# Indexed stores of routed outputs, and a written order from the last dense blocks through the second attention

## The chip, the cores and the metric

The kernel runs on one core of one Trainium2 chip. A core has five engines that run at the same time: TensorE (PE in the profile, with PEld for its weight loads), VectorE (DVE), ScalarE (ACT), GpSimd (POOL) and SyncE (SP), and 16 DMA engines that all of them share. Each engine works through its own queue in order and waits on semaphores that other engines or transfers raise. The metric is the time of one execution on the device in microseconds (us); the median of three runs before the change is 994.7 us.

## The reference, cut to what matters

Two layers of a gated cross-attention block with mixtures of experts, on 16 sequences of 112 tokens of width 256, in fp32. What the change touches is the end of the first layer's feed-forward and the second layer's attention:

```python
x = x + tanh(g_xattn[0]) * L0_xattn(layernorm(x), ctx)
x = x + tanh(g_ffn[0]) * L0_ffn(layernorm(x))     # 14 routed experts, top 2, and 2 shared ones
x = x + tanh(g_xattn[1]) * L1_xattn(layernorm(x), ctx)
x = x + tanh(g_ffn[1]) * L1_ffn(layernorm(x))

def _L0_ffn_ref(x, router_w, rms_w, w1, w2, rms_w_s, w1_s, w2_s):
    gates = softmax(xf @ router_w);  top_v, top_i = top_k(gates, 2)
    masked = zeros.at[rows, top_i].set(top_v);  masked = masked / (masked.sum(-1) + EPS)
    # _ffn: silu(rmsnorm(x) * rw @ W1) @ W2, with W1 256x512 and W2 512x256
    routed_out = einsum('end,ne->nd', vmap(_ffn)(rms_w, w1, w2), masked)
    shared = vmap(_ffn)(rms_w_s, w1_s, w2_s).sum(0)
    return routed_out + shared

def _L1_xattn_ref(x, ctx, ...):          # one head of 256, 112 queries on 375 keys
    attn = softmax((x @ Wq.T + bq) @ (ctx @ Wk.T + bk).T * scale)
    return (x + attn @ (ctx @ Wv.T + bv)) @ Wo.T + bo
```

## The kernel before

The 1792 tokens lie in 14 token tiles of 128 (`NT`), each a row of `x_sb[:, i, :]`, which holds the running sum x on the chip. Tokens normalized and turned (width on the partitions) stand in `xT`. The program has these stages in order.

The first attention ends with a norm per token tile (`normed1`), whose rows go to a table in DRAM, `xn_rows`, beside being turned into `xT`. It is put down in a written order: inside `tc.manual_schedule()` each engine's instructions keep the order of the program text. Everything after it, up to the end, is ordered by a scheduler that places instructions by its own estimates; SP's, POOL's and all other queues are then fixed in that order.

The routed stage sorts the 3584 token-expert pairs by expert into 41 tiles of 128 slots (`TILES0`), each tile of one expert, with the last slots of an expert's last tile and the tail tiles empty. `places` gives for each token the two slots (`at_i`) and for each tile its expert (`owner_i`); `takers` gives for each slot its token, through a matrix product of one-hot rows (0 where a slot is empty). While these are worked out, PE does three units of the two shared experts ("dense" units: an expert `e`, a first token tile `t0`, a width of 4 or 2 tiles; `hidden_piece` makes one of four 128-row pieces of the hidden layer, `output_piece` the output of one token tile and adds it to `x_sb`).

A routed tile `t` then takes: a load of the expert's weights (`wr_sb`, 1025 KB, four buffers, SP's queue), a gather of its tokens' rows (`xg_sb`, an indirect DMA from POOL's queue, four buffers), two PE transposes (`px`), DVE's scaled copy `xgT`, 16 matmuls and a SiLU on ACT (`routed_hidden`), matmuls into `pyr`, DVE's copy `yr` (three buffers), and a plain store of 128 KB to the tile's own slice of a DRAM table `yg` on SP's queue. PE works on the hidden layer of tile t before the output of tile t - 1, and the gather and turn of tile t + 1 before both.

Then come the four dense units that are left (`rest`, two of four token tiles, two of two), with `combine` between them: for each token tile two indirect gathers from `yg` on POOL's queue (`yb`, eight buffers), one for each of the token's two slots, each followed by a DVE instruction that adds the gated rows to `x_sb`, and then the tile's mean and variance (`stats_of`). After all 14, `power` on POOL makes the reciprocal roots of all tiles at once (`rstd2`).

The second attention begins with products of its weights (`product`, `column`, and rows of the biases through `spread`), then `transposed` normalizes and turns all token tiles in pairs, and `add_bias_rows` adds the output bias to `x_sb` on POOL. The loop over the sequences has, in step n, `scores1(n)`, the loads of context n + 2, `apply1(n - 2)`, query products for the next four sequences, `project1` for token tiles that are complete, and `turn1(n - 1)`; `scores1` ends with the division by the softmax sum. The last stage, four experts on all tokens, begins with the same bulk norm and turn (`mv3`, `rstd3`).

The indexed gather that the sum uses today:

```python
nc.gpsimd.indirect_dma_start(
    out=y, out_offset=None, in_=yg,
    in_offset=bass.IndirectOffsetOnAxis(ap=at_i[:, i, r : r + 1], axis=0),
)
```

Of the kernel before, what the change touches and what calls it, by code (L numbers as in the profile page):

```python
# [8 lines left out]
F32 = mybir.dt.float32  # L9
I32 = mybir.dt.int32  # L10
# [41 lines left out]
def tile_flamingo(  # L52
# [103 lines left out]

    tokens_i = const.tile([P, NT], I32, tag="tokens_i", name="tokens_i")
    nc.gpsimd.iota(tokens_i, pattern=[[P, NT]], base=0, channel_multiplier=1)
    tokens = const.tile([P, NT], F32, tag="tokens", name="tokens")
    nc.vector.tensor_copy(tokens, tokens_i)  # L160
    dram = ctx.enter_context(tc.tile_pool(name="dram", bufs=1, space=bass.MemoryType.DRAM))
    xn_rows = dram.tile([N, D], F32, tag="xn_rows", name="xn_rows")
    yg = dram.tile([TILES0 * P, D], F32, tag="yg", name="yg")
    tg = const.tile([P, 4], F32, tag="tg", name="tg")
# [47 lines left out]
    def top2(pool, logits, e, tiny, scale):  # L212
# [34 lines left out]
        if scale is not None:  # L247
            nc.vector.tensor_scalar(sm, sm, scale, None, ALU.mult)
        gates = pool.tile([P, NT, 2], F32, tag=f"gates{e}", name="gates", bufs=1)
        for r in range(2):  # L250
# [68 lines left out]
    def takers(wk, pool, tag, at_i, e, n):  # L319


        def full(name, shape, dtype=F32):
            return wk.tile(shape, dtype, tag=f"{name}{e}", name=name, bufs=1)

        parts = []
        for name, op, by in (("lane", ALU.bitwise_and, P - 1), ("tile", ALU.arith_shift_right, 7)):
            t_i = full(f"{name}_i", [P, NT, 2], I32)
            nc.vector.tensor_scalar(t_i, at_i, by, None, op)
            t = full(name, [P, NT, 2])
            nc.vector.tensor_copy(t, t_i)  # L330
            parts.append(t)
        lane, tile_ = parts
        number = full("number", [P, NT, 2, n])
        sh = [P, NT, 2, n]
        nc.vector.tensor_tensor(
            number, marks[:, :n].unsqueeze(1).unsqueeze(1).to_broadcast(sh), bc(tile_, sh), ALU.is_equal
        )
        nc.vector.tensor_tensor(
            number, number, tokens.unsqueeze(2).unsqueeze(3).to_broadcast(sh), ALU.mult
        )  # L340
        pn = pool.tile([P, n], F32, tag=tag, name="pn")
        for i in range(NT):
            here = wk.tile([P, 2, P], F32, tag="here", name="here", bufs=3)
            for r in range(2):
                nc.vector.tensor_scalar(here[:, r, :], lanes, lane[:, i, r : r + 1], None, ALU.is_equal)
            for r in range(2):
                nc.tensor.matmul(
                    pn, here[:, r, :], number[:, i, r, :],
                    start=(i == 0 and r == 0), stop=(i == NT - 1 and r == 1),
                )  # L350
        taker = full("taker", [P, n], I32)
        nc.vector.tensor_copy(taker, pn)
        return taker

# [78 lines left out]
    with tc.tile_pool(name="a0", bufs=2) as a0, tc.tile_pool(  # L433
# [338 lines left out]
    with tc.tile_pool(name="f0", bufs=3) as f0, tc.tile_pool(  # L772
# [40 lines left out]
        def routed_out(t, w, hT):  # L813
# [27 lines left out]

        def combine(i):
            for r in range(2):
                y = f0.tile([P, D], F32, tag="yb", name="yb", bufs=8)
                nc.gpsimd.indirect_dma_start(
                    out=y, out_offset=None, in_=yg,
                    in_offset=bass.IndirectOffsetOnAxis(ap=at_i[:, i, r : r + 1], axis=0),
                )
                nc.vector.scalar_tensor_tensor(
                    x_sb[:, i, :], y, gates[:, i, r : r + 1], x_sb[:, i, :], ALU.mult, ALU.add  # L850
                )
            stats_of(mv2, i, x_sb[:, i, :])

        units = [(e, t0, w) for t0, w in blocks for e in range(ES)]
# [9 lines left out]
        run(first, route)  # L864
        (at_i, owner_i), taker = found["at"], found["taker"]

# [11 lines left out]

        done = 0

        def added(n):

            nonlocal done
            while n > 0 and done < rest[n - 1][1]:
                combine(done)
                done += 1

        run(rest, added)
        while done < NT:
            combine(done)  # L890
            done += 1

# [3 lines left out]
    rstd2 = by_token("rstd2")  # L896
    power(rstd2, mv2[:, :, 1], EPS, -0.5)
    mv3 = mv_tile("mv3")
    with tc.tile_pool(name="a1", bufs=2) as a1, tc.tile_pool(
        name="a1_mm", bufs=3, space=PSUM  # L900
    ) as ps_mm, tc.tile_pool(name="a1_s", bufs=2, space=PSUM) as ps_s, tc.tile_pool(
        name="a1_t", bufs=1, space=PSUM
    ) as ps_t, tc.tile_pool(name="a1_o", bufs=2, space=PSUM) as ps_o:
        oT = keep.tile([P, KD, N], F32, tag="oT", name="oT1")
        rows_c = {}
# [31 lines left out]
        def spread(bias):  # L937
# [4 lines left out]
            return t  # L942

        for b in range(2):
            context(b)
            context_rows(b)
        wqk = product("wqk", wq1_sb, wk1_sb)
        wvo = product("wvo", wv1_sb, wo1_sb)
# [16 lines left out]

        xT = transposed(ps_mm, "mm", mv2, rstd2)
        add_bias_rows(1)

        G = 4
        qts = {}  # L970

        def queries1(b0, c):
# [3 lines left out]
            for k in range(KD):  # L976
                nc.tensor.matmul(
                    pq, wqk[:, k, c * P : (c + 1) * P], xT[:, k, b0 * TQ : (b0 + G) * TQ],
                    start=(k == 0), stop=(k == KD - 1),
                )  # L980
# [4 lines left out]
        def scores1(b):  # L985
            ps = ps_s.tile([TQ, 512], F32, tag="s", name="ps1")
            t0 = (b % G) * TQ
            for k in range(KD):
                nc.tensor.matmul(
                    ps[:, S : S + 1], xT[:, k, b * TQ : (b + 1) * TQ], wqb[:, k : k + 1],  # L990
                    start=(k == 0), stop=(k == KD - 1),
# [43 lines left out]
        def project1(i):  # L1035
            po = ps_mm.tile([P, D], F32, tag="mm", name="po1")
            cut = slice(i * P, (i + 1) * P)
            for n, (a, w) in enumerate(((xT, wo1_sb), (oT, wvo))):
                for k in range(KD):
# [263 lines left out]
```

## Time and profile before

| what | value |
|---|---|
| median of three runs | 994.7 us (990.64 to 995.96) |
| the profiled execution: time | 990.7 us |
| its span, first to last instruction | 989.0 us |
| mean granted TensorE clock in it | 0.980 |
| PE busy | 928.2 us (94%) |
| DVE, ACT, POOL busy | 493.9, 320.3, 184.8 us |
| routed tiles on PE, about | 404.7 to 573.5 us |
| rest of dense blocks | 573.3 to 629.4 us |
| products, norm, turn | 629.2 to 651.7 us |
| second attention | 651.7 to 737.5 us |
| last stage | 738 us to the end |

The span is shorter than the time by 1.7 us, which lie before the first and after the last instruction. Times of stages are read from PE's timeline, counted from the start of the span. "Busy" of PE counts a matmul at half clock like one at full clock, so a busy PE can still be slow; the granted clock of each stretch says which it is. An engine's idle time is listed with what ended it, its releaser; a releaser that the trace doesn't have is called "remote" or "another core or an unknown queue". The profile's row for the routed gathers (op count, busy time and mean ns, then idle time and what ended it) shows the form in which such groups are given:

```profile
L786 POOL DMA_INDIRECT xg_sb<-xn_rows,taker x41 | 39.0, 952 | 165.6 <-PE px L793 121.4
```

### The profile page before, as it was taken

How to read it: one execution, taken by the hardware profiler on the slowest of the kernel's cores; microseconds unless marked ns; L12 is line 12 of the kernel's file. 1: busy time of each engine (PE TensorE's matmuls, PEld its weight loads, DVE VectorE, ACT ScalarE, POOL GpSimd, SP SyncE). 2: the span in 40 equal slices, each digit the busy share in tenths (PEclk: the TensorE clock that was granted, in tenths of full speed). 3: DMA queues.
4: the chain of work that ended last, by engine and by line, in shares of the span. 5: the costliest groups of instructions: out<-in, count | busy, mean ns of one | idle time of the engine just before them, and what ended most of it. 6: DMA issues, size and time to landing. Idle time of an engine off the chain costs nothing.

```text
span 989.0 us, 18177 instructions
## 1 busy us (share of the span) xinstructions
PE 928.2 (94%) x7306; PEld 666.2 (67%) x7306; DVE 493.9 (50%) x1281; ACT 320.3 (32%) x723; POOL 184.8 (19%) x325
## 2 busy tenths in 40 slices
PE   6999999999999789999989996999989999999995
PEld 3566666666666457888878854768876666766664
DVE  4666665555566165222222233644445655465674
ACT  3555555555554330111111120142223221222222
POOL 3232221111111201222212054410015000000043
PEclk9999999999999999999999997889998999999998
DMA  6400001110110005499999822334400000000011
GB/s 244 161 3 22 23 23 34 33 39 1 59 39 23 11 6 192 130 314 330 303 319 284 296 83 88 127 92 158 124 18 1 0 22 22 1 1 0 1 35 40
DMA packets 34307, 91.51 MB, mean 93 GB/s; under 512 B 4288, under 2 KB 17984, under 8 KB 28976
## 3 DMA queue, kind: packets, MB, share of 16 engines
q1 hardware_dynamic: 30368, 80.79, 24.7%
q0 software_dynamic: 3312, 9.05, 3.2%
q8 instruction: 57, 0.93, 0.4%
q10 hardware_dynamic: 544, 0.52, 0.2%
q14 instruction: 26, 0.21, 0.1%
HBM read 81.31 MB, written 9.04 MB: 91 GB/s over the span
## 4 chain that ended last, share of the span: by engine, by line
PE 82%; DMA 8%; DVE 3%; ACT 3%; another core or an unknown queue 2%; issue 1%; POOL 0%; POOLq 0%; DVEq 0%; ACTq 0%
PE ph L1130 10%; PE py L1160 9%; DMA wr_sb<-in_wr_dram 8%; PE pt L573 6%; PE pt L592 6%; PE pt L472 5%; PE sp L545 5%; PE phr L805 5%; PE pyr L817 4%; PE ph L407 4%; PE py L417 3%; PE sp L485 3%; PE po L1040 2%; PE ps L994 2%; PE pa L1029 2%
## 5 line engine op out<-in xcount | busy, mean ns | idle before, releaser
L552 DVE TENSOR_REDUCE mz<-sp 112x2 f32<-112x750 f32 x128 | 114.2, 934 | 55.7 <-PE sp L545 55.7
L580 ACT ACTIVATE pT<-pt 125x336 f32<-125x336 f32 x256 | 94.6, 456 | 65.0 <-PE pt L573 65.0
L1130 PE MATMUL ph<-w1b_sb,xT 128*128 128x512 f32 x224 | 102.1, 600 | 0.0
L1160 PE MATMUL py<-w2b_sb,hT 128*128 128x256 f32 x448 | 100.8, 382 | 0.0
L805 PE MATMUL phr<-xgT,wr_sb 128*128 128x128 f32 x656 | 82.5, 279 | 11.4 <-DVE xgT L795 11.3
L1160 PEld LDWEIGHTS py<-w2b_sb,hT 128*128 128x128 f32 x448 | 82.2, 190 | 14.0 <-ACT hT L1152 4.2
L805 PEld LDWEIGHTS phr<-xgT,wr_sb 128*128 128x128 f32 x656 | 77.2, 191 | 15.3 <-DVE xgT L795 15.1
L795 DVE TENSOR_SCALAR xgT<-px,wr_sb 128x128 f32<-128x128 f32 x82 | 24.9, 346 | 109.2 <-DMA wr_sb<-in_wr_dram 93.9
L817 PE MATMUL pyr<-wr_sb,hTr 128*128 128x256 f32 x328 | 77.4, 379 | 0.0
L810 ACT ACTIVATE hTr<-phr 128x512 f32<-128x512 f32 x41 | 24.5, 597 | 155.5 <-PE phr L805 155.5
L1130 PEld LDWEIGHTS ph<-w1b_sb,xT 128*128 128x128 f32 x224 | 41.7, 191 | 42.4 <-issue 38.7
L786 POOL DMA_INDIRECT xg_sb<-xn_rows,taker x41 | 39.0, 952 | 165.6 <-PE px L793 121.4
L188 POOL TENSOR_SCALAR rstd<-mv 128x1 f32<-128x1 f32 (+2 forms) x23 | 5.2, 228 | 338.4 <-DVE mv L181 338.4
L592 PEld LDWEIGHTS pt<-pT,va 125*32 125x32 f32 x1536 | 38.0, 109 | 39.1 <-ACT pT L580 33.6
L817 PEld LDWEIGHTS pyr<-wr_sb,hTr 128*128 128x128 f32 x328 | 59.3, 190 | 6.4
L573 PE MATMUL pt<-qm,kt 32*125 32x112 f32 x1536 | 61.2, 283 | 0.7 <-ACT kt L477 0.4
L592 PE MATMUL pt<-pT,va 125*32 125x112 f32 x1536 | 58.7, 264 | 2.0 <-ACT pT L580 2.0
L573 PEld LDWEIGHTS pt<-qm,kt 32*125 32x125 f32 x1536 | 49.1, 183 | 15.7 <-issue 11.6
L1137 ACT ACTIVATE rh<-mvh,eps 128x1 f32<-128x1 f32 x56 | 16.3, 292 | 131.4 <-DVE mvh L181 131.3
L545 PE MATMUL sp<-kt,qt 32*112 32x375 f32 x512 | 55.9, 488 | 1.2 <-ACT qt L504 0.8
L472 PE MATMUL pt<-ctx_sb,wk 128*128 128x375 f32 x128 | 50.3, 516 | 5.8 <-DMA ctx_sb<-in_ctxT_dram 5.8
L417 PE MATMUL py<-w_sb,hT 128*128 128x256 f32 x192 | 44.3, 390 | 7.2 <-issue 7.2
(241 smaller groups left out, 1447.5 us busy)
## 6 DMA issues: line engine op xcount, KB each, us to landing
wr_sb<-in_wr_dram SPq DMA_DIRECT2D x41, 1025.0 KB
ctx_sb<-in_ctxT_dram SPq DMA_DIRECT2D x32, 375.0 KB
ctxn_sb<-in_ctxN_dram SPq DMA_DIRECT2D x16, 375.0 KB
yg<-yr SPq DMA_DIRECT2D x41, 128.0 KB
w1b_sb<-in_w1b_dram SPq DMA_DIRECT2D x4, 512.0 KB
w2b_sb<-in_w2b_dram SPq DMA_DIRECT2D x4, 512.0 KB
xn_rows<-xn SPq DMA_DIRECT2D x14, 128.0 KB
out_dram<-yf SPq DMA_DIRECT2D x14, 128.0 KB
```

Of the source, the lines that this page charges most:

```text
L407: nc.tensor.matmul(ph, a[:, k, m * P : (m + 1) * P], xT[:, k, t0 * P : (t0 + n) * P], start=(k == 0), stop=(k == KD - 1),)
L417: nc.tensor.matmul(py, hT[:, m, j * P : (j + 1) * P], c[:, m, :], start=(m == 0), stop=(m == KH - 1),)
L472: nc.tensor.matmul(pk, wk0_sb[:, k, c * P : (c + 1) * P], ctxs[b][:, k, :], start=(k == 0), stop=(k == KD - 1),)
L545: nc.tensor.matmul(sps[j // 2][:TQ, j % 2, :S], qt[r : r + HP, c, t0 : t0 + TQ], kt[r : r + HP, g, u, :], start=True, stop=True,)
L552: nc.vector.tensor_reduce(mz[:, 2 * h : 2 * h + 2, HD * (1 - u)], sp[:TQ, :, :S], AX.X, ALU.max, negate=True,)
L573: nc.tensor.matmul(sts[j][:SC, s * TQ : (s + 1) * TQ], kt[r : r + HP, c // 2, c % 2, s * SC : (s + 1) * SC], qm[r : r + HP, :], start=True ...
L580: nc.scalar.activation(pT[:, j, :], sts[j][:SC, : NSC * TQ], AF.Exp)
L592: nc.tensor.matmul(po[r : r + HP, :], va[:, s, (c // 2) * 8 + j * 2 + c % 2, :], pT[:, j, s * TQ : (s + 1) * TQ], start=(s == 0), stop=(s ...
L805: nc.tensor.matmul(ph[:, m, :], a[:, k, m * P : (m + 1) * P], xgT[:, k, :], start=(k == 0), stop=(k == KD - 1),)
L817: nc.tensor.matmul(py, hT[:, m, :], c[:, m, :], start=(m == 0), stop=(m == KH - 1))
L1130: nc.tensor.matmul(ph, xT[:, k, i * P : (i + 1) * P], a[:, k, :], start=(k == 0), stop=(k == KD - 1),)
L1160: nc.tensor.matmul(py, hT[:, m, j * P : (j + 1) * P], c[:, m, :], start=(m == 0), stop=(m == KH - 1),)
```

## The change

There are three parts.

Routed outputs are stored by index. A table `pairs` holds, for token n and choice r, the number 2n + r + 1; `takers` now yields `slot`, this number for each slot (0 for an empty one), and from it `taker`, the token plus one. `xn_rows` gets a row 0 of zeros for empty slots, its tokens move down by one row. The output of a routed tile goes to `y_rows` at the rows `slot` names, by an indirect DMA from POOL's queue in place of SP's plain store; empty slots all write row 0. The two rows of a token then lie beside each other, and `combine` loads those of a whole token tile with one plain DMA of 256 KB on SP's queue (`yb`, now 2 KB per partition, six buffers).

The rest of the dense units, the sums, the norms and the second attention stand in one written order, within `tc.manual_schedule()`. The products and bias rows come first. Then the dense pieces follow in the order hidden 0, hidden 1, output 0, output 1, hidden 2, hidden 3, output 2, output 3 (28 pieces), and after every second piece from the third on a `tick(c)`: sum and root of token tile c, norm of tile c - 1 on DVE, turn of tile c - 2 on PE with ACT's copy and POOL's bias add. Ticks 13 to 15 come among the first two query products. The turned tokens stand in `xs`, in the buffer of `oT`, since `xT` is still read by the dense pieces; `oT` takes that of `xT`.

In the attention's loop the division by the softmax sum leaves `scores1` and becomes `divided(n)`, put down after `project1` and before `turn1(n - 1)`.

```diff
@@ constants
-    tokens_i = const.tile([P, NT], I32, tag="tokens_i", name="tokens_i")
-    nc.gpsimd.iota(tokens_i, pattern=[[P, NT]], base=0, channel_multiplier=1)
-    tokens = const.tile([P, NT], F32, tag="tokens", name="tokens")
-    nc.vector.tensor_copy(tokens, tokens_i)
+    pairs_i = const.tile([P, NT, 2], I32, tag="pairs_i", name="pairs_i")
+    nc.gpsimd.iota(pairs_i, pattern=[[2 * P, NT], [1, 2]], base=1, channel_multiplier=2)
+    pairs = const.tile([P, NT, 2], F32, tag="pairs", name="pairs")
+    nc.vector.tensor_copy(pairs, pairs_i)
+    zeros = const.tile([1, D], F32, tag="zeros", name="zeros")
+    nc.gpsimd.memset(zeros, 0.0)
...
-    xn_rows = dram.tile([N, D], F32, tag="xn_rows", name="xn_rows")
-    yg = dram.tile([TILES0 * P, D], F32, tag="yg", name="yg")
+    xn_rows = dram.tile([N + 1, D], F32, tag="xn_rows", name="xn_rows")
+    y_rows = dram.tile([2 * N + 1, D], F32, tag="y_rows", name="y_rows")
@@ takers
-            number, number, tokens.unsqueeze(2).unsqueeze(3).to_broadcast(sh), ALU.mult
+            number, number, bc(pairs, sh), ALU.mult
...
-        taker = full("taker", [P, n], I32)
-        nc.vector.tensor_copy(taker, pn)
-        return taker
+        slot, taker = full("slot", [P, n], I32), full("taker", [P, n], I32)
+        nc.vector.tensor_copy(slot, pn)
+        nc.vector.tensor_scalar(taker, pn, 1.0, None, ALU.add)
+        nc.vector.tensor_scalar(taker, taker, 1, None, ALU.arith_shift_right)
+        return slot, taker
@@ first attention
-            nc.sync.dma_start(out=xn_rows[i * P : (i + 1) * P, :], in_=xns[i])
+            nc.sync.dma_start(out=xn_rows[1 + i * P : 1 + (i + 1) * P, :], in_=xns[i])
...
+        at(9, 3, lambda: nc.sync.dma_start(out=xn_rows[0:1, :], in_=zeros))
@@ routed_out
-            nc.sync.dma_start(out=yg[t * P : (t + 1) * P, :], in_=y)
+            nc.gpsimd.indirect_dma_start(
+                out=y_rows, out_offset=bass.IndirectOffsetOnAxis(ap=slot[:, t : t + 1], axis=0),
+                in_=y, in_offset=None,
+            )
@@ after the routed tiles
-        run(rest, added)
-        while done < NT:
-            combine(done)
-            done += 1
...
-    power(rstd2, mv2[:, :, 1], EPS, -0.5)
     mv3 = mv_tile("mv3")
+    written = ExitStack()
+    written.enter_context(tc.manual_schedule())
...
-        oT = keep.tile([P, KD, N], F32, tag="oT", name="oT1")
+        xs = keep.tile([P, KD, N], F32, tag="oT", name="xT1")
...
+        def combine(i):
+            y = a1.tile([P, 2, D], F32, tag="yb", name="yb", bufs=6)
+            rows = y_rows[1 + 2 * i * P : 1 + 2 * (i + 1) * P, :]
+            nc.sync.dma_start(out=y, in_=rows.rearrange("(p r) d -> p r d", r=2))
+            for r in range(2):
+                nc.vector.scalar_tensor_tensor(
+                    x_sb[:, i, :], y[:, r, :], gates[:, i, r : r + 1], x_sb[:, i, :],
+                    ALU.mult, ALU.add,
+                )
+            stats_of(mv2, i, x_sb[:, i, :])
+            power(rstd2[:, i : i + 1], mv2[:, i, 1:2], EPS, -0.5)
...
+        def normed2(i):
+            xns[i] = work.tile([P, D], F32, tag="xn1", name="xn2", bufs=2)
+            nc.vector.tensor_scalar(
+                xns[i], x_sb[:, i, :], mv2[:, i, 0:1], rstd2[:, i : i + 1],
+                ALU.subtract, ALU.mult,
+            )
+
+        def turned2(i):
+            pt = ps_s.tile([P, KD, P], F32, tag="s", name="ptx")
+            xn = xns.pop(i)
+            for k in range(KD):
+                nc.tensor.transpose(pt[:, k, :], xn[:, k * P : (k + 1) * P], ident)
+            nc.scalar.copy(xs[:, :, i * P : (i + 1) * P], pt)
+            nc.gpsimd.tensor_add(x_sb[:, i, :], x_sb[:, i, :], rowsg[:, 1, :])
...
+        def tick(c):
+
+            if c < NT:
+                combine(c)
+            if 0 <= c - 1 < NT:
+                normed2(c - 1)
+            if 0 <= c - 2 < NT:
+                turned2(c - 2)
...
-        xT = transposed(ps_mm, "mm", mv2, rstd2)
-        add_bias_rows(1)
-
+        order = [hidden(0), hidden(1), output(0), output(1), hidden(2), hidden(3), output(2), output(3)]
+        ticks, n = {3 + 2 * c: c for c in range(13)}, 0
+        for phase in order:
+            for f, args in phase:
+                f(*args)
+                n += 1
+                if n in ticks:
+                    tick(ticks[n])
+        oT = keep.tile([P, KD, N], F32, tag="xT", name="oT1")
@@ scores1
+            return p, sm
+
+        def divided(p, sm):
             rs = a1.tile([TQ, 1], F32, tag="rs1", name="rs1")
@@ the loop
-        for c in range(KD):
-            queries1(0, c)
+        for c in range(13, NT + 2):
+            tick(c)
+            if c - 13 < KD:
+                queries1(0, c - 13)
...
+            if n < B:
+                ps[n] = divided(*ps[n])
             if 0 <= n - 1 < B:
                 pTs[n - 1] = turn1(ps.pop(n - 1))
+    written.close()
```

More of the change, by code (lines that the diff above doesn't have):

```diff
@@ L248, in top2 @@
             nc.vector.tensor_scalar(sm, sm, scale, None, ALU.mult)
-        gates = pool.tile([P, NT, 2], F32, tag=f"gates{e}", name="gates", bufs=1)
+        gates = keep.tile([P, NT, 2], F32, tag=f"gates{e}", name="gates")
         for r in range(2):
@@ L840, in run @@
                 prev = (hT, e, t0, w)
[L842 to L852, printed above, removed]
         units = [(e, t0, w) for t0, w in blocks for e in range(ES)]
@@ L864, in tile_flamingo @@
         run(first, route)
-        (at_i, owner_i), taker = found["at"], found["taker"]
+        (_, owner_i), (slot, taker) = found["at"], found["taker"]
         ready = routed_in(0)
@@ L877, in tile_flamingo @@
         routed_out(*prev)
[L879 to L884, printed above, removed]
-                combine(done)
-                done += 1
-        run(rest, added)
-        while done < NT:
-            combine(done)
-            done += 1
     rstd2 = by_token("rstd2")
-    power(rstd2, mv2[:, :, 1], EPS, -0.5)
     mv3 = mv_tile("mv3")
+    written = ExitStack()
+    written.enter_context(tc.manual_schedule())
     with tc.tile_pool(name="a1", bufs=2) as a1, tc.tile_pool(
@@ L942, in spread, with h_bank, y_bank @@
             return t
+        def h_bank():
+            return ps_mm.tile([P, 512], F32, tag="mm", name="ph")
+        def y_bank():
+            return ps_o.tile([P, 512], F32, tag="av", name="py")
+        def combine(i):
[9 more added lines that the diff above has]
+            power(rstd2[:, i : i + 1], mv2[:, i, 1:2], EPS, -0.5)
+        xns = {}
+        def normed2(i):
[11 more added lines that the diff above has]
+            nc.gpsimd.tensor_add(x_sb[:, i, :], x_sb[:, i, :], rowsg[:, 1, :])
         for b in range(2):
@@ L946, in tile_flamingo, with hidden, output @@
             context_rows(b)
+        hTs = {}
+        def hidden(u):
+            hTs[u] = hidden_rows()
+            for m in range(KH):
+                yield hidden_piece, (h_bank, hTs[u], *rest[u], m)
+        def output(u):
+            for j in range(rest[u][2]):
+                yield output_piece, (y_bank, hTs[u], *rest[u][:2], j)
+        def tick(c):
[5 more added lines that the diff above has]
+                turned2(c - 2)
         wqk = product("wqk", wq1_sb, wk1_sb)
@@ L977, in queries1 @@
                 nc.tensor.matmul(
-                    pq, wqk[:, k, c * P : (c + 1) * P], xT[:, k, b0 * TQ : (b0 + G) * TQ],
+                    pq, wqk[:, k, c * P : (c + 1) * P], xs[:, k, b0 * TQ : (b0 + G) * TQ],
                     start=(k == 0), stop=(k == KD - 1),
@@ L989, in scores1 @@
                 nc.tensor.matmul(
-                    ps[:, S : S + 1], xT[:, k, b * TQ : (b + 1) * TQ], wqb[:, k : k + 1],
+                    ps[:, S : S + 1], xs[:, k, b * TQ : (b + 1) * TQ], wqb[:, k : k + 1],
                     start=(k == 0), stop=(k == KD - 1),
@@ L1037, in project1 @@
             cut = slice(i * P, (i + 1) * P)
-            for n, (a, w) in enumerate(((xT, wo1_sb), (oT, wvo))):
+            for n, (a, w) in enumerate(((xs, wo1_sb), (oT, wvo))):
                 for k in range(KD):
```

## The prediction

> **What bounds the kernel now.** I read the page first (where the slices are not full), then the windows by stage, the waits, the chain, and last the timelines of the engines in the stretch the change rewrites. TensorE (PE) is busy 94% of the span, so the question is where the other 6%, and the half-speed time inside the 94%, lie. The windows (first column the stretch, second its length, then PE busy; PEclk is the granted clock):
>
> ```profile
> 420.00:560.00 140.00, 129.01 (x865) 116.81 (x864) 32.01 (x99) 20.30 (x34) 29.29 (x31) 1.00 0.95 312
> ...
> 592.40:599.60 7.20, 0.01 (x1) 0.00 (x0) 4.33 (x14) 0.00 (x0) 5.42 (x6) 0.71 0.37 101
> 599.60:605.70 6.10, 6.09 (x14) 4.90 (x15) 0.00 (x0) 0.00 (x0) 4.58 (x6) 0.50 0.36 104
> 605.70:611.00 5.30, 1.65 (x8) 0.97 (x6) 0.76 (x2) 0.46 (x2) 0.41 (x1) 1.00 0.14 43
> ...
> 636.10:651.70 15.60, 12.97 (x46) 8.03 (x46) 8.23 (x14) 4.73 (x8) 10.41 (x14) 0.56 0.21 81
> 651.70:737.50 85.80, 85.78 (x497) 68.95 (x495) 39.03 (x135) 27.00 (x72) 0.00 (x0) 1.00 0.35 108
> ```
>
> The routed tiles (first row) move 312 GB/s with the DMA engines 95% busy: 34 tiles (ACT's 34) in 140 us, 4.1 us each. The attention (last row) is a full PE. The loss is between: PE stops at 592.4, runs at half clock to 605.7, stops again, and at 636.1 to 651.7 is slow once more. The waits and the chain name the first hole:
>
> ```profile
> ACT hT L411 <- remote: 22.7, 1, 22.7
> ...
> DVE x_sb L421 <- remote: 10.7, 1, 10.7
> ```
> ```profile
> 587.87 22.59 another core or an unknown queue
> ```
>
> "Remote" is a wait whose releaser the trace doesn't show. The timelines of PE and POOL show what stood there:
>
> ```profile
> 587.07 5.34 PE L417 MATMUL py<-w_sb,hT 128*128 128x256 f32 x24
> 599.61 3.78 PE L417 MATMUL py<-w_sb,hT 128*128 128x256 f32 x8 [7.20 <-issue]
> ...
> 607.40 0.38 PE L407 MATMUL ph<-xT,w_sb 128*128 128x256 f32 x1 [0.45 <-issue]
> 610.98 1.13 PE L407 MATMUL ph<-xT,w_sb 128*128 128x256 f32 x4 [3.20 <-ACT hT L411]
> ```
> ```profile
> 576.41 0.94 POOL L845 DMA_INDIRECT yb<-yg,at_i  x1 [26.29 <-DMA yg<-yr]
> 577.66 0.95 POOL L845 DMA_INDIRECT yb<-yg,at_i  x1 [0.30 <-issue]
> ```
>
> PE filled the three `py` banks and waited for VectorE (DVE), whose first L421 was queued behind sixteen gathered sums (599.11). Its next three waited to 610.24, while POOL issued gathers every 1.25 us until 606.1. Both releases come about 4 us after the last gather of the burst; I read them as its doing, which the trace suggests and doesn't prove.
>
> **What the Trainium skill says.** "DMA: Bandwidth & Descriptors", section "Two DMAs through the same engine are not ordered": only a completion semaphore orders two DMAs. All 41 new stores name the whole of `y_rows`, so I expect each to wait for the landing of the one before; stores to `yg` went to separate slices and show no such wait. The same page, "Anatomy of one DMA — SWDGE (gpsimd) path", puts a fixed 2.0 us on such a transfer; the trace agrees roughly (gather at 576.41, first sum at 579.16: 2.75 us). "TensorE: Matmul & The Clock Gate", "Part 1: The HAM clock gate", has half rate after an idle window of about 3.4 us, and "Part 4: PE-mode transpose" that transposes don't count as busy; the 0.50 after 7.2 us of idling and the 0.56 among the transposes fit both.
>
> **The change part by part.** The sums are against the profiled execution: span 989.0 us, time 990.7 us.
>
> 1. *Rest of dense blocks, norms, transposes: 573.3 to 651.7, 78.4 us.* The work in it at full clock, from timeline rows: 8 hidden pieces over four token tiles 13.9 (L407 x32, 13.90) and their 8 outputs 13.8 (L417 x32 is 6.9); 8 hidden pieces over two tiles 6.9 and their 4 outputs 6.9; products and bias rows 6.9 (629.2 to 636.1); 28 transposes 3.1; the first queries 3.0; two score biases 0.8. Sum 55.3; lost 23.1 (10.85 in three gaps, 3.0 to the half clock before 605.7, the rest after 636.1). Afterwards the products come first, then 28 pieces with a tick (sum, norm, turn) after every second one. New waits: DVE writes the `spread` rows in order behind copies that wait for PE, twice about 0.8 = 1.6. In the half-size hidden pieces PE needs 2 x 0.86 + 0.43 = 2.15 per tick, DVE two sums 0.97, stats 0.43, 0.18, norm 0.54 = 2.12 plus hand-overs: I take 1.5 for these and for the last turn. The one-column products at the start may cost a half-clock window of 3.4 us: I take half its 3.4 loss, 1.7. That gives 55.3 - 0.8 + 4.8 = 59.3: 19.1 saved. POOL's per-token power (0.22 + 0.57) and bias add (0.73) fit under a tick.
>
> 2. *Second attention, 85.8 us with PE full.* The written order has the same work plus 0.8 (score biases of the first two sequences, earlier done before 651.7). `divided` and `turn1` lie an iteration apart, so DVE's 1.2 + ACT's 0.8 + DVE's 0.6 are covered by about 5 us of PE. At the end `apply1(15)` comes straight behind `turn1(15)` and waits for ACT's copy (0.44 and hand-over): 0.9; at the start 0.5. Together -2.2: 16.9 saved. The next stage begins as now.
>
> 3. *Small edits.* Two more DVE operations in `takers` (about 0.2 each) delay gathers that PE first needs 14 us later (387.7 against 404.7): nothing. `zeros` and the longer iota on POOL hide in its 0.78 us wait before the first `rstd`: up to 0.2. The zero row is one small DMA on SP's queue at step 9: nothing.
>
> 4. *The stores on POOL.* They leave SP's queue, where each followed a weight load, and add 41 x 1.25 = 51 us to POOL, which had 35 of 170 busy. Behind a waiting store stand POOL's gathers; PE waits for those. DVE's `yr` (three buffers) waits for stores landed. Bytes are the same. Alone a link of the chain takes 2.75 + 0.1 = 2.9 us, under the 4.1 of a tile. Under load, by the packet records, a gather's last packet comes 5.0 to 8.5 us after its issue, 6.6 in the mean. So a link costs between 2.9 and 7; a store that starts when the last has landed meets a load part done, and I take 4.8. It falls 0.7 behind per tile, 28 us over 41; four gathers, three `yr` and three PSUM banks absorb some five tiles (21 us), and a slower tile eases the DMA engines. I take 4 us in the stage. At its end some five stores remain, 14.5 us, then 2.5 for the first plain load and 2.9 for sum, power and norm: 20; PE has 6.9 + 1.6 + 13.9 x 7/8 = 20.7 of other work before the first turn. I take 1.5 for this, 1 for costlier packets: 6.5 (bounds: -3, since SP's stores held that queue up to 2.27 us; +35 if a link costs 5.2 or more). Repeated rows: padding all goes to row 0; "Rules for kernel authors" of the DMA page says that one writer's data lands, nothing of time, and no run here shows it.
>
> Net 16.9 - 0.2 - 6.5 = 10.2: 990.7 goes to 980.5. The median shown, 994.7, lies 4.0 above that execution; from there it would be 984.5. I say **982**.
>
> **The rivals.** *Forecast, chained stores mostly absorbed*: 974 to 990, chance 0.45. For it: 2.9 unloaded is under 4.1.
>
> *No chain, or one that stays under a tile*: costs of part 4 go to 0 or 1; 977. For it: SP's queue is freed; against: the stores' common target. Chance 0.20.
>
> *The chain sets the tile*: a link of 5.2 us costs 41 x 1.1 = 45, less some 20 absorbed and 3 more at the end: 28 where I took 6.5, so about 1004, slower than before. It decides from a link of about 4.9 us on, where it eats the 16.9. For it: gathers at 6.6 under load, DMA 95% busy; against: a slower tile unloads the engines. Chance 0.17.
>
> *The written order gives it back*: DVE falls behind the ticks, or PE stands on a hand-over of each iteration (0.5 x 16 = 8 us); gain 2 to 5, about 991. For it: PE has no idle time in the attention now, so any wait counts; against: the slack counted in part 2. Chance 0.18.
>
> **How the numbers follow.** Forecast 982, own range 974 to 990. For 8 in 10 I take 970 (no chain, full clock) to 1003 (most of the third case). Within 0.5% is about what can be told from no change here, 5 us. Faster: 0.42 + 0.20 + 0.04 = 0.66; same: 0.03 + 0.11 = 0.14; slower: 0.17 + 0.03 = 0.20.
>
> **What would show it.** Right: no "remote" wait near 600, PE full through the dense pieces, no granted clock of 0.5 but one window behind the bias products, attention at 87 to 89 us; routed tiles of 4.1 to 4.3 us with POOL's stores waiting on a store's landing. Wrong: no such wait (then nearer 977); tiles of 4.5 us or more, PE waiting for `px` or `pyr` banks; DVE's first sum waiting for a plain load long after the last tile; gaps on PE each iteration of the attention.

## The result, and the profile after

The change makes the kernel slower: 1031.4 us in the median of four runs (1030.72 to 1039.76) against 992.7 before (four runs, one more than in the median of 994.7 above), a ratio of 1.041 with a 95% interval of 1.034 to 1.047. The prediction was 982. The profiled execution of the changed kernel took 1030.8 us, with a span of 1029.1. Some executions of a kernel ran slower as a whole at a lower granted clock; medians and ratios, here and below, leave them out.

The same four stretches as before, from PE's timeline (end of the last routed output; first scores; last `po`, the second attention's last output; end). The third row is an experiment told below, the changed kernel without the order among its stores:

| kernel | to the last routed output | to the first scores | second attention | last stage | span |
|---|---|---|---|---|---|
| before | 573.3 | 78.4 | 85.8 | 251.5 | 989.0 |
| changed | 608.2 | 77.4 | 88.3 | 255.2 | 1029.1 |
| changed, stores in no order | 570.7 | 62.1 | 88.3 | 254.8 | 975.9 |

Up to the last routed output 34.9 us are lost, and the stretch of dense blocks and norms, which was to win 19.1, wins 1.0. The windows of the changed kernel show both (stretch, its length, busy time of PE, PEld, DVE, ACT, POOL, granted clock, DMA share, GB/s):

```profile
420.00:560.00 140.00, 116.77 (x721) 105.44 (x720) 26.32 (x83) 16.72 (x28) 49.92 (x51) 0.93 0.77 259
608.20:685.60 77.40, 59.85 (x237) 43.81 (x237) 35.70 (x96) 12.90 (x31) 25.66 (x45) 0.87 0.40 117
685.60:773.90 88.30, 87.10 (x506) 70.04 (x504) 37.99 (x135) 27.11 (x73) 0.73 (x2) 1.00 0.34 105
773.90:1029.10 255.20, 237.79 (x984) 162.31 (x984) 146.54 (x384) 68.08 (x145) 36.81 (x48) 0.96 0.04 12
```

In the first row ACT made 28 hidden layers in 140 us where it made 34 before (its count in the same stretch): a tile takes 5.0 us, not 4.1. The DMA engines, 95% busy before, have 23% to spare, so bandwidth isn't what holds the tiles. The page's groups and the list of waits name what does (a wait: total, times, longest):

```profile
L827 DVE COPY yr<-pyr 128x256 f32<-128x256 f32 x41 | 17.4, 424 | 153.1 <-DMA y_rows<-yr,slot 130.5
L828 POOL DMA_INDIRECT y_rows<-yr,slot x41 | 40.5, 989 | 126.5 <-DVE yr L827 108.2
```
```profile
DVE yr L827 <- DMA y_rows<-yr,slot: 130.5, 31, 8.5
...
PE phr L813 <- DVE xgT L803: 33.8, 16, 5.4
...
PE pw L905 <- DVE wqk L909: 14.6, 1, 14.6
DVE wqk L909 <- DMA y_rows<-yr,slot: 11.6, 1, 11.6
```

A copy that takes 0.42 us waits 130.5 us in total for the landing of stores. PE doesn't wait for this copy; it waits 33.8 us for `xgT`, the next tile's tokens, which no store has anything to do with. DVE's timeline (start, duration, instruction, idle time before it and what ended it), and below it PE's, show why:

```profile
462.50 0.42 DVE L827 COPY yr<-pyr 128x256 f32<-128x256 f32 x1 [3.95 <-DMA y_rows<-yr,slot]
462.84 0.60 DVE L803 TENSOR_SCALAR xgT<-px,wr_sb 128x128 f32<-128x128 f32 x2
468.31 0.42 DVE L827 COPY yr<-pyr 128x256 f32<-128x256 f32 x1 [4.87 <-DMA y_rows<-yr,slot]
468.66 0.60 DVE L803 TENSOR_SCALAR xgT<-px,wr_sb 128x128 f32<-128x128 f32 x2
...
613.03 0.42 DVE L827 COPY yr<-pyr 128x256 f32<-128x256 f32 x1 [3.61 <-DMA y_rows<-yr,slot]
625.08 0.76 DVE L909 COPY wqk<-pw 128x256 f32<-128x256 f32 x2 [11.62 <-DMA y_rows<-yr,slot]
```
```profile
467.33 0.38 PE L801 MATMUL px<-ident,xg_sb 128*128 128x128 f32 x2
469.05 2.09 PE L813 MATMUL phr<-xgT,wr_sb 128*128 128x128 f32 x16 [1.33 <-DVE xgT L803]
...
609.95 1.03 PE L905 MATMUL pw<-wo,wv 128*128 128x256 f32 x4
625.56 2.08 PE L905 MATMUL pw<-wo,wv 128*128 128x256 f32 x4 [14.58 <-DVE wqk L909]
```

PE has turned the next tokens at 467.71, but DVE's queue is in order: `xgT` stands behind a `yr` that has no free buffer until 468.31, and PE starts the tile 1.33 us late. The Trainium skill says this of the engine ("Perfetto Trace Analysis", "Tensor Engine Instruction (MATMUL, LD_WEIGHTS)": ACT, DVE and GpSimd are strict FIFO), and the trace agrees. The last four lines, two of each engine, show the second hole: after the routed tiles PE stops for 14.58 us in the weight products, because DVE's copy of a product isn't made until the last store, issued at 621.58, has landed.

That the stores wait for each other is seen best at the end of POOL's timeline. The page's row puts the wait of most stores down to `yr`, but with three buffers that copy, made for a tile two further on, waits for the same landing and is only the later to end. The last copy is made at 613.03 and the next store at 613.64; two more follow with no copy left to wait for, still 4.1 and 3.9 us apart:

```profile
617.71 0.97 POOL L828 DMA_INDIRECT y_rows<-yr,slot  x1 [3.09 <-DMA y_rows<-yr,slot]
621.58 0.97 POOL L828 DMA_INDIRECT y_rows<-yr,slot  x1 [2.90 <-issue]
```

Call the time from one store's start to the next a link. The first store starts at 412.52; the 34 links up to 599.24 are 186.7 us, so one takes 5.49; the last six, when the weight loads are over, take 3.2 to 4.1.

### The profile page after: what moved, and what is told of

Same layout as the page of the kernel before. It is cut to its first block, busy times and chain, and to the rows that moved or that the text cites. A ratio compares the mean times of both kernels' runs of the same rounds, so it can differ in the third digit from the quotient of the medians.

```text
span 1029.1 us, 18142 instructions
## 1 busy us (share of the span) xinstructions
PE 938.5 (91%) x7306; PEld 676.2 (66%) x7306; DVE 490.9 (48%) x1283; ACT 321.1 (31%) x730; POOL 209.4 (20%) x365
## 5 line engine op out<-in xcount | busy, mean ns | idle before, releaser
L813 PE MATMUL phr<-xgT,wr_sb 128*128 128x128 f32 x656 | 89.2, 293 | 33.9 <-DVE xgT L803 33.8
L813 PEld LDWEIGHTS phr<-xgT,wr_sb 128*128 128x128 f32 x656 | 83.2, 204 | 38.4 <-DVE xgT L803 38.2
L827 DVE COPY yr<-pyr 128x256 f32<-128x256 f32 x41 | 17.4, 424 | 153.1 <-DMA y_rows<-yr,slot 130.5
L818 ACT ACTIVATE hTr<-phr 128x512 f32<-128x512 f32 x41 | 24.5, 597 | 190.2 <-PE phr L813 158.0
L192 POOL TENSOR_SCALAR rstd<-mv 128x1 f32<-128x1 f32 (+2 forms) x36 | 9.2, 255 | 364.7 <-DVE mv L185 364.7
L825 PE MATMUL pyr<-wr_sb,hTr 128*128 128x256 f32 x328 | 82.2, 397 | 0.0
L825 PEld LDWEIGHTS pyr<-wr_sb,hTr 128*128 128x128 f32 x328 | 63.3, 203 | 7.8
L828 POOL DMA_INDIRECT y_rows<-yr,slot x41 | 40.5, 989 | 126.5 <-DVE yr L827 108.2
L599 PEld LDWEIGHTS pt<-pT,va 125*32 125x32 f32 x1536 | 38.0, 109 | 39.1 <-ACT pT L587 33.6
```

What stands on the lines that cost most here:

```text
L599: nc.tensor.matmul(po[r : r + HP, :], va[:, s, (c // 2) * 8 + j * 2 + c % 2, :], pT[:, j, s * TQ : (s + 1) * TQ], start=(s == 0), stop=(s ...
L813: nc.tensor.matmul(ph[:, m, :], a[:, k, m * P : (m + 1) * P], xgT[:, k, :], start=(k == 0), stop=(k == KD - 1),)
L825: nc.tensor.matmul(py, hT[:, m, :], c[:, m, :], start=(m == 0), stop=(m == KH - 1))
L828: nc.gpsimd.indirect_dma_start(out=y_rows, out_offset=bass.IndirectOffsetOnAxis(ap=slot[:, t : t + 1], axis=0), in_=y, in_offset=None,)
```

## The experiments

Each ratio is to the kernel before, run on the same chip, with its 95% interval.

**The order among the stores taken away.** Empty slots get a row of their own behind the tokens' rows, so that no two stores write the same row, and the stores are declared to have nothing in common, so that none waits for another:

```diff
+    spare = const.tile([P, TILES0], F32, ...)      # 2N + 1 + slot number
-    y_rows = dram.tile([2 * N + 1, D], ...)
+    y_rows = dram.tile([2 * N + 1 + TILES0 * P, D], ...)
...
+        nc.vector.scalar_tensor_tensor(own, pn, 0.0, spare[:, :n], ALU.is_equal, ALU.mult)
+        nc.vector.tensor_tensor(own, own, pn, ALU.add)
-        nc.vector.tensor_copy(slot, pn)
+        nc.vector.tensor_copy(slot, own)
...
-            nc.gpsimd.indirect_dma_start(
+            put = nc.gpsimd.indirect_dma_start(
...
+            tc.declare_no_dep(put.ins, group="rows", reason="own rows")
+            tc.add_to_no_dep_group("rows", put.ins)
```

> The changed kernel, but every empty slot has a row of its own behind the tokens' rows, so that no two indexed stores share a row and none has to wait for another. If the order among the stores is what costs: routed tiles back to 4.1 to 4.3 us each (168 to 176 us for the 41), no 14.6 us gap among the weight products, about 976 to 982 us in all, faster than before and after. If indexed stores on POOL's queue cost by themselves (descriptors, single rows, POOL's queue): tiles stay near 4.9 us and the time above 1010. If the written order costs: above 992 though the tiles recover.

Measured: 980.1 us, ratio 0.990 (0.987 to 0.993): 1% faster than the kernel before, and far faster than the changed one. Its waits and its windows:

```profile
PE phr L820 <- DVE xgT L810: 9.4, 16, 1.2
...
PE pw L914 <- DVE wqk L918: 1.3, 1, 1.3
```
```profile
420.00:560.00 140.00, 131.93 (x884) 119.26 (x883) 33.46 (x103) 20.31 (x34) 63.63 (x65) 1.00 0.92 318
570.70:632.80 62.10, 57.87 (x237) 42.09 (x237) 35.26 (x95) 12.89 (x30) 22.88 (x43) 0.95 0.49 141
```

The 34 tiles are back, the hole is 1.3 us, and no `yr` copy waits for a store. The two profiled spans differ by 53.2 us (1029.1 less 975.9). Of these, 1.8 lie before the first store (412.5 here, 410.7 there; the granted clock up to 400 us was 0.98 and 1.00), so they aren't the stores' doing. The order among the stores therefore costs 51.4: 35.7 more up to the last routed output, 13.3 in the products' hole (14.6 less 1.3), 2.0 behind it at a lower clock, 0.4 in the rest.

**Stores alone, in the old order.** The kernel before, with the change's tables, stores and plain loads, and all else left to the scheduler (`yb` with three buffers):

```diff
-            nc.sync.dma_start(out=yg[t * P : (t + 1) * P, :], in_=y)
+            nc.gpsimd.indirect_dma_start(
+                out=y_rows, out_offset=bass.IndirectOffsetOnAxis(ap=slot[:, t : t + 1], axis=0),
+                in_=y, in_offset=None,
+            )
```

> The kernel before with indexed stores and plain loads, the rest in the scheduler's order (yb with three buffers). If the order among the stores is the cause: tiles near 4.9 us (about 200 us for the 41), and dense pieces behind DVE's last copies; 1010 to 1035 us, about like the changed kernel or worse, as the gain of the written order (some 16 us) is missing. If the written order is the cause: 985 to 995.

Measured: 1033.0, ratio 1.045 (1.039 to 1.050). `yr` waits 135.3 us for stores and PE 33.6 us for `xgT`, as in the whole change. The loss belongs to the stores, whatever order follows.

**The written order alone.** The changed kernel with plain stores to the tiles' own slices on SP, and in `combine` two indexed gathers in place of the plain load:

```diff
+            nc.sync.dma_start(out=yg[t * P : (t + 1) * P, :], in_=y)
...
-            nc.sync.dma_start(out=y, in_=rows.rearrange("(p r) d -> p r d", r=2))
+            for r in range(2):
+                nc.gpsimd.indirect_dma_start(
+                    out=y[:, r, :], out_offset=None, in_=yg,
+                    in_offset=bass.IndirectOffsetOnAxis(ap=at_k[:, i, r : r + 1], axis=0),
+                )
```

> The changed kernel with the old exchange: plain stores to slices of yg on SP, and in each tick two indexed gathers on POOL. It has the written order alone. If the order among the indexed stores is the cause: tiles 4.1 us, 970 to 982 us in all, the gathers spread over the ticks (1.25 us each, two per 3.9 us of PE). If the burst of gathers was the cause of the unexplained wait near 600 us and the ticks don't thin it out: gaps of some 10 us again, 982 to 992. If the written order costs: above 992.

Measured: 1038.7, ratio 1.051 (1.045 to 1.057): a miss. The routed tiles are as before; the ticks are slow. Its waits and POOL's timeline:

```profile
DVE x_sb L943 <- DMA yb<-yg,at_i: 72.5, 28, 7.0
...
PE ptx L963 <- DVE xn L954: 42.5, 13, 6.3
```
```profile
593.86 0.29 POOL L192 TENSOR_SCALAR rstd<-mv 128x1 f32<-128x1 f32 x1 [5.99 <-DVE mv L185]
594.23 0.57 POOL L194 TENSOR_TENSOR rstd<-rstd,roots 128x1 f32<-128x1 f32 x1
594.99 1.08 POOL L938 DMA_INDIRECT yb<-yg,at_i  x1 [0.19 <-issue]
596.38 0.94 POOL L938 DMA_INDIRECT yb<-yg,at_i  x1 [0.30 <-issue]
600.45 0.29 POOL L192 TENSOR_SCALAR rstd<-mv 128x1 f32<-128x1 f32 x1 [3.12 <-DVE mv L185]
```

In a written order the gathers of a token tile stand in POOL's queue behind the root of the tile before, which waits for DVE's statistics, which wait for the gather before. Nothing is fetched ahead, though six buffers are there.

**The same with the gathers ahead.** Four token tiles' gathers before the products, and in tick c those of tile c + 4:

```diff
+            if c + 4 < NT:
+                fetch(c + 4)
...
+        for i in range(4):
+            fetch(i)
         wqk = product("wqk", wq1_sb, wk1_sb)
```

> The run of the written order alone (plain slice stores, two indexed gathers for a token tile) came out at 1039; here the same with the gathers of a token tile issued four ticks ahead of its sums, the first four before the products. Theory, that run lost its time because a gather stood in GpSimd's queue behind the root and the bias add of the tick before, so that each tick waited for a gather just issued: now 974 to 988, no waits of PE for xn over 1.5 us. Rival 1, gathers disturb PE or DVE as in the kernel before (waits of an unknown releaser): 988 to 1000. Rival 2, the written order itself is the loss: 1025 or more.

Measured: 987.7, ratio 0.992 (0.990 to 0.994), some 50 us from moving 28 gathers in one queue. PE's wait for `xn` falls from 42.5 to 6.8 us:

```profile
PE ptx L968 <- DVE xn L959: 6.8, 6, 2.0
```

The longest single one, 2.0, is above the 1.5 expected, and the time lies at the upper end of the theory's 974 to 988. The written order itself isn't a loss.

**Ten `yr` buffers.**

```diff
-            y = f0.tile([P, D], F32, tag="yr", name="yr")
+            y = f0.tile([P, D], F32, tag="yr", name="yr", bufs=10)
```

> The changed kernel with ten yr buffers in place of three; all else as it is. Theory, the chain of stores has a length of its own (41 links of 4.9 us, last landing near 620) and the three buffers only decide where PE pays for it: the routed tiles go back to 4.1 us (PE's last pyr near 575 to 585 where it was 608), but the first sum still waits for the last landing, so a hole of 20 to 30 us opens on PE at the first turn (ptx); time 1005 to 1022. Rival, the price is the back-pressure through VectorE's queue alone: with it gone the time is 975 to 990. Third: faster tiles load the DMA engines again, a link grows to 5.2 us or more, and the time stays at 1022 to 1036.

Measured: 1034.3, ratio 1.046 (1.040 to 1.052). No wait of `yr` for a store is left, as it should be, and yet the tiles don't go back to 4.1 us: ACT makes 29 hidden layers in the 140 us from 420. POOL's timeline and PE's:

```profile
511.37 0.99 POOL L828 DMA_INDIRECT y_rows<-yr,slot  x1 [4.97 <-DVE xgT L803]
512.66 0.97 POOL L794 DMA_INDIRECT xg_sb<-xn_rows,taker  x1 [0.30 <-issue]
518.92 0.99 POOL L828 DMA_INDIRECT y_rows<-yr,slot  x1 [5.29 <-DMA y_rows<-yr,slot]
520.21 0.97 POOL L794 DMA_INDIRECT xg_sb<-xn_rows,taker  x1 [0.30 <-issue]
```
```profile
513.05 1.89 PE L825 MATMUL pyr<-wr_sb,hTr 128*128 128x256 f32 x8
520.69 0.69 PE L801 MATMUL px<-ident,xg_sb 128*128 128x128 f32 x2 [5.75 <-DMA xg_sb<-xn_rows,taker]
```

Store and gather alternate in POOL's queue, so a waiting store holds back the gather behind it. PE now waits 24.5 us for gathered tokens and 16.8 in the products. My theory had missed this second queue, so its time fell; the time of the third case was met, but a link didn't grow for it: by the starts of the stores it is 5.26 us here, 5.49 in the changed kernel (the 4.9 in this expectation and the next ones I had read too low, from single links). The last store is issued at 617.4, 4.2 us earlier than with three buffers.

**Own rows for the empty slots, order kept.** As in the first experiment, without the declaration:

```diff
-        nc.vector.tensor_copy(slot, pn)
+        nc.vector.tensor_copy(slot, own)
```

> The changed kernel with a row of its own in y_rows for each empty slot, in place of row 0 for all of them; the stores still wait for each other. Theory, a link is a landing (issue, descriptors, packets, completion): it stays at 4.7 to 5.0 us, time 1025 to 1037. Rival, writes of many packets to the one row 0 queue up in memory and make the link long: a link falls to 4.2 us or less, time 978 to 995.

Measured: 1028.2, ratio 1.041 (1.035 to 1.047). The first 34 links take 5.41 us in the mean, so row 0 isn't what makes them long. It also shows that in the first experiment the declaration did the work, and not the rows.

**One place for all, without an index.**

```diff
-            nc.gpsimd.indirect_dma_start(
-                out=y_rows, out_offset=bass.IndirectOffsetOnAxis(ap=slot[:, t : t + 1], axis=0),
-                in_=y, in_offset=None,
-            )
+            nc.gpsimd.dma_start(out=y_rows[1 : 1 + P, :], in_=y)
...
-            rows = y_rows[1 + 2 * i * P : 1 + 2 * (i + 1) * P, :]
+            rows = y_rows[1 : 1 + 2 * P, :]
```

> The changed kernel with plain stores on GpSimd's queue, all to the same 128 rows of y_rows, and loads that read the same rows for every token tile (the routed sums then don't take each token's own outputs). The chain stays, the index goes. Theory, what costs is the wait for the landing: 4 to 4.8 us a link, time 1000 to 1032, with the same waits of VectorE's yr copies. Rival, the indexed store is what is slow[...]: links of 3 us, under a tile's 4.1, no wait of yr worth naming, time 976 to 988.

Measured: 1015.0, ratio 1.022 (1.019 to 1.024). The first 34 links are 5.32 us in the profiled execution, where 4 to 4.8 were expected, and `yr` waits 123.8 us for them. (That execution took 1032.8, but it was late before any store: its first one starts at 424.6, 12.1 us later than in the changed kernel.) The waiting for a landing is what costs; the index adds little under load.

**Without the weight loads.**

```diff
+            if t >= 4:
+                w = held[t % 4]
+            else:
+                w = held[t] = f0.tile([P, WR], F32, tag="wr", name="wr_sb", bufs=4)
...
+            if t < 4:
+                nc.sync.dma_start(out=w, in_=wr[bass.ds(e, 1)]...)
```

> The changed kernel with weights loaded for the first four routed tiles only; the later tiles take those again (37 loads of 1 MB left out, so the routed outputs aren't the reference's). The chain of stores stays. Theory, a link is a landing that other DMA traffic lengthens: without the weight loads it falls to 3 to 4 us, PE sets the tile at about 3.9 us, time 975 to 995. Rival, a link costs its 4.9 us whatever else moves: PE waits as before, time 1022 to 1036.

Measured: 972.2, ratio 0.977 (0.971 to 0.983). The order is kept, but 38 tiles fit in 140 us and PE never stops:

```profile
420.00:560.00 140.00, 140.00 (x981) 130.56 (x980) 35.36 (x113) 22.69 (x38) 70.25 (x72) 1.00 0.24 69
```

Stores start every 3.73 us, at PE's pace, so a link is no longer than that. So the 5.5 us of the changed kernel are a landing among 1 MB loads.

**The products in other memory.** Why does DVE's copy of a product wait for the last store at all? Its target comes from the pool that follows the routed stage's in the program and takes over its memory. Here the products, columns, spread rows and score bias lie in memory that lasts:

```diff
-            t = a1.tile([P, KD, D], F32, tag=name, name=name, bufs=1)
+            t = keep.tile([P, KD, D], F32, tag=name, name=name)
```

> The changed kernel, its chain untouched, with the weight products, their columns, the spread rows and the score bias in memory that lasts through the program, in place of the pool that takes over the routed stage's memory. In the changed kernel PE stands 14.6 us in the products, for a copy of VectorE that waits until the last store has landed (625), although its last yr copy is done at 613.5. Theory, that copy's target lies where yr buffers lay, which the last stores still read: with another place the copy runs behind the last yr copy, the hole shrinks to 2 to 4 us, and the first sum still finds its rows landed before PE comes to the first turn: 1015 to 1022. Rival 1, the sums take the place of the copy as what waits for the last landing: a hole of about 10 us at the first turn, 1026 to 1034. Rival 2, the copy waits for the store itself, wherever its target lies: hole and time stay, 1026 to 1040.

Measured: 1027.7, ratio 1.035 (1.031 to 1.040). It lies 3.7 us under the change, but the two intervals overlap; what became of the hole is read from the traces. DVE's timeline and PE's:

```profile
612.34 0.42 DVE L827 COPY yr<-pyr 128x256 f32<-128x256 f32 x1 [3.48 <-DMA y_rows<-yr,slot]
612.68 0.74 DVE L909 COPY wqk<-pw 128x256 f32<-128x256 f32 x2
...
636.52 1.00 DVE L943 SCALAR_TENSOR_TENSOR x_sb<-yb,gates,x_sb 128x256 f32<-128x256 f32 x2 [15.01 <-DMA yb<-y_rows]
```
```profile
613.15 1.13 PE L905 MATMUL pw<-wo,wv 128*128 128x256 f32 x4 [2.68 <-DVE wqk L909]
...
640.12 0.69 PE L963 MATMUL ptx<-ident,xn 128*128 128x128 f32 x2 [5.13 <-DVE xn L954]
```

The copy now runs straight behind the last `yr`, and the hole shrinks from 14.58 to 2.68: that cause is shown. But the first sum takes over the wait. The last store is issued at 620.73; the plain loads start at 625.3 on SP, behind three context loads that waited too, and the sum runs only at 636.52, 11.2 us after the start of its load, so PE stands 5.13 us at the first turn. The theory of the hole was right and its time wrong; rival 1 gave the time, with half its hole. To the first scores, 4.8 us are won: 11.9 in the hole and 0.5 before it, less 5.1 at the turn and some 2.5 to a lower granted clock (0.81, 0.83 and 0.79 in three windows from 606 to 650).

**A better version?** The stores without order, and in it the one-column bias products behind the first four hidden pieces:

```diff
+        late = {1: bias_bqk, 2: bias_wqb, 3: bias_bb, 4: bias_rows}
...
+                if n in late:
+                    late[n]()
                 if n in ticks:
```

> The run without the chain (own rows for empty slots, stores declared to touch no common row), and in it the one-column bias products behind the first four hidden pieces instead of ahead of all pieces. There the window behind these products had a granted clock of 0.70 and then 0.91. Theory, one-column products let the clock gate fall: spread among hidden pieces they don't, 2 to 4 us less than the same run without this: about 977. Rival, the clock falls from something else (the stop for the product's copies): same time within 1 us.

> The run without the chain once more, on the same chip as the one with the bias products moved, to compare the two: 978 to 983.

Measured: 978.3, ratio 0.984 (0.980 to 0.988), and 979.1, ratio 0.986 (0.983 to 0.988), for the same without this edit. The same stretch in each, with the edit and without:

```profile
582.00:592.00 10.00, 10.00 (x42) 6.07 (x41) 1.20 (x8) 2.39 (x4) 0.00 (x0) 1.00 0.86 224
```
```profile
582.00:592.00 10.00, 9.09 (x33) 5.74 (x33) 1.75 (x9) 1.19 (x2) 0.00 (x0) 0.83 0.84 226
```

In this one execution of each the granted clock stays full with the edit, as the theory has it, but the times differ by 0.8 us and the intervals overlap: the expected gain of 2 to 4 us isn't shown. Either is 1.5% faster than the kernel before.

## Why the prediction was wrong

*The rest of the dense blocks (19.1 saved) was nearly right, where the stores let it be.* Without the order among the stores the stretch takes 62.1 us where 59.3 were worked out; the clock of 0.70 and then 0.91 around and behind the one-column products cost at most 3.5 (0.30 of 8.5 us and 0.09 of 10) where 1.7 was taken. No "remote" wait is left. *The attention (88.0) was right*: 88.3, with two hand-overs of 0.58 before its last `apply1` and no gap that comes in each iteration. *The small edits* show nothing. "The next stage begins as now" was off by a little: the last stage does the same work and is 3.7 us longer; its first 15.2 us after PE's stop were granted 0.63 where the kernel before had 0.78, which makes 2.3 of it. Why the clock is lower there isn't shown.

*The stores (6.5) were wrong*, and nearly all that the change lost lies there: the mechanism was named, each store waiting for the landing of the one before, but it cost 51.4, beyond the part's own bound of 35. (For a link of 5.2 the rival's own sum has 28, so the two prices didn't agree either.) Three terms of the sum failed.

First, "I take 4.8" for a link: measured 5.49 under load (and 3.15, not 2.9, alone). The bounds (2.9 and 7) held it. The mean landing of a gather that stood beside them, 6.6, pointed the right way; I lowered it by a judgement with no row behind it. With 5.49 a tile falls 1.4 behind, not 0.7. "A slower tile eases the DMA engines" happened (0.95 to 0.77 busy) and wasn't enough; only when the weight loads were left out did a link fit under a tile.

Second, "four gathers, three `yr` and three PSUM banks absorb some five tiles (21 us)" and "I take 4 us in the stage". From the first store to the last it is 209.1 us, in the run without order 160.9: 48.1 us of lag, nearly all of the 51.4. The buffers put off some 12 us of it (the last store is issued 13.4 us after PE's last routed output, without order 0.9), the tiles paid 35.7, and the hole in the products then charged what was put off. The count added buffers as if each could fill by itself. But the instruction that finds no buffer also stops what is queued behind it: `yr` stops `xgT` on DVE, and with ten buffers the store stops the gather on POOL. The prediction had named the gathers behind a waiting store and never asked what stands behind a waiting `yr`.

Third, the 20.7 us "of other work before the first turn" that were to cover the last landings. PE had that work and couldn't do it: the products, first in the written order, waited for memory that the last stores still read. And where they don't (the run with other memory), the turn waits instead. There a term on the other side shows: "2.5 for the first plain load" was 11.2 in that run, and 12.4 from issue to landing in the run without order, where the first five loads are issued together beside loads of contexts; later single ones there take 2.6 to 2.9.

The rival that came true is *the chain sets the tile*. That the chain would set the tile was right. Its 1004 was too low because it kept the same "some 20 absorbed", and for the same reason its point of decision, a link of 4.9, was too high: with nothing absorbed in the end, 0.3 us a link over a tile's 4.1 eats the 13.1 us of span that the run without order gains (an estimate: 13.1 over 40 links).

## What to carry to other kernels

When transfers are made to wait for each other, compare the loaded landing time, not the unloaded one, with the pace of the loop; if it is longer, expect nearly the whole difference times the count to be paid, as here, and the buffers to choose only where. For each instruction that such a wait can stop, read on in its engine's queue: what stands behind it is stopped too, and so is whatever takes over the memory that the last transfers read. In a written order put the issue of a fetch as far ahead as its buffers allow, since no scheduler will move it past an unrelated wait.

## What the runs showed of the hardware

Writing one row 128 times costs more than 128 rows. Counted from the reference's routing, 36 tiles hold tokens and the last five are empty slots alone. In the changed kernel the links behind stores of tiles with tokens end at 3.16 and 3.29 us, those behind empty ones, all to row 0, take 3.87 to 4.07; with own rows the empty ones take 3.14 to 3.19. POOL's timeline at the end of the changed kernel, then with own rows:

```profile
602.40 0.97 POOL L828 DMA_INDIRECT y_rows<-yr,slot  x1 [2.18 <-DVE yr L827]
605.69 0.97 POOL L828 DMA_INDIRECT y_rows<-yr,slot  x1 [2.31 <-DVE yr L827]
609.62 0.97 POOL L828 DMA_INDIRECT y_rows<-yr,slot  x1 [2.96 <-DVE yr L827]
613.64 0.97 POOL L828 DMA_INDIRECT y_rows<-yr,slot  x1 [3.05 <-DVE yr L827]
```
```profile
605.87 0.97 POOL L835 DMA_INDIRECT y_rows<-yr,slot  x1 [2.19 <-DVE yr L834]
609.01 0.97 POOL L835 DMA_INDIRECT y_rows<-yr,slot  x1 [2.18 <-DVE yr L834]
612.16 0.97 POOL L835 DMA_INDIRECT y_rows<-yr,slot  x1 [2.18 <-DMA y_rows<-yr,slot]
```

With little beside it, a plain store of the same 128 KB from POOL follows the last in 2.5 us, an indexed one in 3.15; under the weight loads they take 5.3 and 5.3 to 5.5. Either is then well above a tile's 4.1.
